# First attention of a decoder: compressed contexts as products of 64 rows into two banks, and the output added to the rows in every step

## The chip, the cores and the metric

The kernel runs on one core of a Trainium2 chip. The core has five engines that work side by side: PE multiplies matrices, DVE, ACT and POOL work on elements, SP starts transfers. PE writes to PSUM, a memory [...]; DVE and ACT read it from there. The metric is the device time of one execution in microseconds; lower is better. Matrices of f32 go through PE as two instructions for each product, each with a weight load (PEld) and a matmul (PE).

## The reference, cut to what matters

The program is a two-layer decoder in float32 on 16 blocks of 128 rows with 256 features. Only its first attention is touched. It has 16 heads of 128 features and two sources of values per head: a window of the rows around a query, and the entries, each a weighted mean of four neighbouring rows (32 entries per block), of which the best 8 are kept:

```python
entries = jnp.einsum('bcr,bcrh->bch', w_cmp, hidden_states.reshape(Bq, C, RATIO, HID))
cv = entries @ Wv + bv
...
ctx_sparse = jnp.einsum('bhsk,bhskd->bhsd', pw, v_g)
...
ctx_local = jnp.einsum('bhcqk,bhckd->bhcqd', pl, vw).reshape(Bq, NH, Sq, D)
merged = (ctx_sparse + ctx_local) * 0.5
out = merged.transpose(0, 2, 1, 3).reshape(Bq, Sq, NH * D) @ Wo + bo
```

The result is added to the input rows and normalized. The sum of both contexts and the product with Wo are what the change rearranges.

## The kernel before, in words

The first attention runs in 64 steps, one for each block b of 128 rows and each group hg of four heads, in the order b = 0, hg = 0 to 3, b = 1, and so on. A step's work is spread over four rounds of the loop at L486 and after, so that in one round PE works on four steps at once. PE's order is written out by hand (`manual_schedule` at L492 holds PE's instructions to the order of the program); the order on DVE, ACT and POOL is found by a planner that simulates costs.

In one round PE does, in this order:

1. `normed` with Wlk (L343, its product in `project`, L338): local keys of the new step, 512 columns;
2. `contexts` (L450) of the step that began three rounds ago;
3. `transposed` (L366): eight transposes of keys and queries of the step before, at L373;
4. `normed` with Wq (L338 again);
5. `output` (L461) of the step whose contexts were just made;
6. `scores` (L376), with a mask product at L380 and the scores at L384;
7. `weightsT` (L439): four transposes of the local weights (L442) and one of the compressed weights (L446), for the step that began two rounds ago;
8. `values` (L361): the product with Wlv;
9. now and then work on the entries (`entry_values` at L322 and others).

The compressed values of a block are kept in `cvz` (L271), a tile with four slots of 128 rows, one for each head. Slot h is zero but for rows 32h to 32h + 31, which hold the values of the 32 entries (written at L332). The compressed weights of four heads are transposed together: `pcT` (L445 to L448) has the 32 entries of head h in rows 32h to 32h + 31. A product of slot h with all 128 rows of pcT so picks the right head, because the other rows meet zeros.

`contexts` makes four accumulations of two products each into the tile `pm`, one PSUM bank with one buffer: for head h the local product (L454), then the compressed one (L455), both over all 128 rows. ACT then copies pm to `mT` in SBUF, times 0.5 (L457).

`output` multiplies mT by the group's rows of Wo (L465), four f32 products of 256 columns. They accumulate in the tile `po`, another bank, over all four groups of a block; only behind the last group DVE adds po to the block's rows `xs[b]` (L473). `output_bias` (L475), once in round 6, makes the part of the output that comes from the bias of the values, also in po's bank, and DVE and POOL add it to bo and all rows (L482, L484).

Of the kernel before, what the change touches and what calls it, by code (L numbers as in the profile page):

```python
# [18 lines left out]
F32 = mybir.dt.float32  # L19
# [3 lines left out]
AF = mybir.ActivationFunctionType  # L23
ALU = mybir.AluOpType
# [3 lines left out]
P = 128  # L28
HID = 256
# [19 lines left out]
def decoder(ctx: ExitStack, tc: tile.TileContext, w: dict, out: bass.AP):  # L49
    nc = tc.nc  # L50
# [12 lines left out]
    xs = [const.tile([P, HID], F32, name=f"x{t}") for t in range(NB)]  # L63
# [28 lines left out]
    def load_row(pool, ap, name, tag=None, bufs=None):  # L92

        n = ap.shape[0]
        kw = {} if tag is None else {"tag": tag, "bufs": bufs}
        t = pool.tile([P, n], F32, name=name, **kw)
        nc.gpsimd.dma_start(out=t, in_=ap.partition_broadcast(P))
        return t
# [73 lines left out]
    NH, D = 16, 128  # L172
    NC4 = P // 4
    NK = NC4 + P
    with ExitStack() as ph:
        pool = ph.enter_context(tc.tile_pool(name="l0a", bufs=1))
        wk = ph.enter_context(tc.tile_pool(name="l0a_k", bufs=2))
        ps = ph.enter_context(tc.tile_pool(name="l0a_ps", bufs=2, space=PSUM))
# [10 lines left out]
        wts, bias = {}, {}  # L189
# [16 lines left out]
        bo = load_row(pool, w["L0_attn_bo"], "bo0")  # L206
# [64 lines left out]
        cvz = [pool.tile([P, 4, D], F32, name=f"cvz{n}") for n in range(3)]  # L271
        for t in cvz:
            nc.gpsimd.memset(t, 0.0)

        def entry_logits(g):
            pl = ps.tile([P, NC4 * 4, 4], F32, tag="proj", name="pl")
            for k in range(2):
                nc.tensor.matmul(
                    pl.rearrange("p c r -> p (c r)"), lhsT=wcmp_b[:, k, :], rhs=xT[g][:, k, :], start=k == 0, stop=k == 1
                )  # L280
            lg = wk.tile([P, P, 4], F32, tag="big0", name="lg", bufs=1)
            nc.vector.tensor_scalar(lg, pl, bcmp, None, ALU.add)
            return lg
# [165 lines left out]

        def contexts(b, st):  # L450

            pm = ps.tile([P, 4, P], F32, tag="pm", name="pm", bufs=1)
            for h in range(4):
                nc.tensor.matmul(pm[:, h, :], lhsT=st["Wlv"][:, h, :], rhs=st["plT"][:, h, :], start=True, stop=False)  # L454
                nc.tensor.matmul(pm[:, h, :], lhsT=cvz[b % 3][:, h, :], rhs=st["pcT"], start=False, stop=True)  # L455
            st["mT"] = wk.tile([P, 4, P], F32, tag="mT", name="mT")
            nc.scalar.activation(st["mT"], pm, AF.Copy, scale=0.5)  # L457

        outs = {}

        def output(b, hg, st):  # L461
            if hg == 0:
                outs[b] = ps.tile([P, HID], F32, tag="po", name="po", bufs=1)
            for h in range(4):
                nc.tensor.matmul(  # L465
                    outs[b],
                    lhsT=st["mT"][:, h, :],
                    rhs=wts["Wo", hg][:, h, :],
                    start=hg == 0 and h == 0,
                    stop=hg == 3 and h == 3,  # L470
                )
            if hg == 3:
                nc.vector.tensor_tensor(xs[b], xs[b], outs.pop(b), ALU.add)  # L473

        def output_bias():  # L475

            pb = ps.tile([P, HID], F32, tag="po", name="pb", bufs=1)
            for h in range(NH):
                rep = wk.tile([P, P], F32, tag="blv_b", name="blv_b")
                nc.gpsimd.tensor_copy(rep, blv[:, h : h + 1].to_broadcast([P, P]))  # L480
                nc.tensor.matmul(pb, lhsT=rep, rhs=wts["Wo", h // 4][:, h % 4, :], start=h == 0, stop=h == NH - 1)
            nc.vector.scalar_tensor_tensor(bo, pb, 0.5, bo, ALU.mult, ALU.add)  # L482
            for t in range(NB):
                nc.gpsimd.tensor_tensor(xs[t], xs[t], bo, ALU.add)  # L484

# [5 lines left out]

        with tc.manual_schedule(engines={mybir.EngineType.PE}):  # L492
            lgs = {0: entry_logits(0)}
            entry_weights(lgs[0])
            for k in range(2):
                entry_sums(0, lgs[0], k)
            for n in range(len(steps) + 6):
# [5 lines left out]
                if fourth:  # L503
                    contexts(fourth[0], fourth[2])
# [12 lines left out]
                if fourth:  # L517
                    output(*fourth)
                if n == 6:
                    output_bias()  # L520
# [9 lines left out]
                g, r = (n + 10) // 16, (n + 10) % 16  # L530
                if 1 <= g < NG:
                    if r == 0:
                        lgs[g] = entry_logits(g)
                    elif r == 1:
                        entry_weights(lgs[g])
                    elif r in (2, 3):
                        entry_sums(g, lgs[g], r - 2)
                    elif r == 4:
                        cks[g] = entry_keys(g)
                    elif r == 6:  # L540
                        entry_keysT(g, cks.pop(g))
# [9 lines left out]
    with ExitStack() as ph:  # L551
# [174 lines left out]
        ps = ph.enter_context(tc.tile_pool(name="l0x_ps", bufs=1, space=PSUM))  # L726
# [225 lines left out]
        def put_out(gp, js, at):  # L952

            if 0 in js:
                pys[gp] = ps.tile([P, 2, HID], F32, tag="misc", name="py")
            output(gp, js, pys[gp])
            for u in range(2):
                if 4 * u + 3 in js:
                    later(at + 1, "DVE", add_output, 2 * gp + u, pys[gp][:, u])
            if 7 in js:  # L960
                later(at + 1, "POOL", norm_pair, gp)
# [82 lines left out]
        with tc.manual_schedule(engines=set(ordered)):  # L1044
            for n in range(len(steps) + 9):
# [11 lines left out]
                for part in range(2):  # L1057
# [8 lines left out]
                    gp, r = n // 16, n % 16  # L1066
                    if part == 1 and 0 < gp <= LAST and r >= 8:
                        ffn_half(gp - 1, r - 8, 1, at)
                    for hh in range(2):

                        q = n - 3 if (n - 3) % 2 == 1 else n - 4
# [260 lines left out]
    with ExitStack() as ph:  # L1332
        pool = ph.enter_context(tc.tile_pool(name="l1a", bufs=1))
        wk = ph.enter_context(tc.tile_pool(name="l1a_k", bufs=2))
        ps = ph.enter_context(tc.tile_pool(name="l1a_ps", bufs=1, space=PSUM))
# [37 lines left out]
        with tc.manual_schedule(engines={mybir.EngineType.PE}):  # L1373
# [4 lines left out]
            for n in range(len(steps) + 16):  # L1378
# [3 lines left out]
                if n in (5, 7):  # L1382
                    q = NB // 2 - 2 + n // 7
# [17 lines left out]
                t, r = n // 4, n % 4  # L1401
# [14 lines left out]
    with ExitStack() as ph:  # L1416
# [3 lines left out]
        ps = ph.enter_context(tc.tile_pool(name="l1x_ps", bufs=1, space=PSUM))  # L1420
# [47 lines left out]
        with tc.manual_schedule(engines={mybir.EngineType.PE}):  # L1468
# [8 lines left out]
            for n in range(len(steps) + 14):  # L1477
# [7 lines left out]
                t, r = n // 2, n % 2  # L1485
# [30 lines left out]
    with ExitStack() as ph:  # L1516
        wk = ph.enter_context(tc.tile_pool(name="l1f_k", bufs=2))
        ps = ph.enter_context(tc.tile_pool(name="l1f_ps", bufs=2, space=PSUM))

        def shares(g, i):  # L1520

            t = wk.tile([P, G], F32, tag="share", name="sh", bufs=6)
            at = 0
            while at < P:
                e = (i * P + at) // IE
                n = min(P - at, (e + 1) * IE - i * P - at)
                nc.sync.dma_start(out=t[at : at + n], in_=share[g][e, :].partition_broadcast(n))
                at += n
            return t

        def gated(g, rows, gate, up, sh=None):

            pgu = []
            for wt, tag in ((gate, "gate"), (up, "up")):
                pp = ps.tile([P, G], F32, tag=tag, name=tag)
                for k in range(2):
                    nc.tensor.matmul(pp[:rows], lhsT=wt[:, k, :], rhs=xT[g][:, k, :], start=k == 0, stop=k == 1)  # L1537
                pgu.append(pp)
            h = wk.tile([P, G], F32, tag="h", name="h", bufs=NI + 3 + 3)
            nc.scalar.activation(h[:rows], pgu[0][:rows], AF.Silu)  # L1540
            nc.vector.tensor_tensor(h[:rows], h[:rows], pgu[1][:rows], ALU.mult)  # L1541
            if sh is not None:
                nc.vector.tensor_tensor(h, h, sh, ALU.mult)
            return h

        for g in range(NG):
            parts = []
            for i in range(3):
                at, rows = i * P, min(P, IS - i * P)
                wsh = moe_w["sh"]  # L1550
                h = gated(g, rows, wsh[:, :, at : at + rows], wsh[:, :, IS + at : IS + at + rows])
                parts.append((h, moe_w["sd"][:rows, i, :], rows))
            for i in range(NI):
                at = slice(i * P, (i + 1) * P)
                h = gated(g, P, moe_w["g"][:, :, at], moe_w["u"][:, :, at], shares(g, i))
# [8 lines left out]
            for i4 in range(4):  # L1564
                t = 4 * g + i4
                py = ps.tile([P, HID], F32, tag="py", name="py")
                for n, (h, wt, rows) in enumerate(parts):
                    nc.tensor.matmul(  # L1568
                        py, lhsT=h[:rows, i4 * P : (i4 + 1) * P], rhs=wt, start=n == 0, stop=n == len(parts) - 1
# [59 lines left out]
```

## Time and profile before

| | |
|---|---|
| median of 3 runs | 2725.06 us (2724.89 to 2730.54) |
| profiled execution, its own time | 2732.66 us |
| its span, first to last instruction | 2730.9 us |
| mean granted TensorE clock | 0.974 |
| busy over the span: PE, PEld, DVE, ACT, POOL | 92%, 55%, 70%, 54%, 44% |
| contexts, L454 and L455: records of PE | 512 each, mean 277 ns |
| output, L465: records of PE | 512, mean 380 ns |
| addition of the output, L473 on DVE | 16, mean 414 ns |
| copy of the contexts, L457 on ACT | 64, mean 591 ns |

The profile names an instruction by engine and line; the operands are given by the program's names. A matmul's record lasts longer than the time for which it keeps the next one off, since matmuls are pipelined: the duration of one is told by its record, the room that it takes by the distance to the next start. In the rows, 128\*128 is the part of the array that a matmul uses (rows\*columns), behind it stand the elements of its output. PEclk, the granted clock, is a share of full speed.

### The profile page before, as it was taken

What the parts mean: (1) busy time and instruction counts of PE and PEld (TensorE: products, weight loads), DVE (VectorE), ACT (ScalarE), POOL (GpSimd) and SP (SyncE); (2) the same over time, 40 slices, a digit from 0 to 9 for tenths busy, and PEclk for the clock granted to TensorE, in tenths of its full rate; (3) what the DMA queues carried; (4) which work ended last, traced back from release to release, by engine and by line L of the source; (5) the groups of instructions that cost most, each with busy time, mean ns of one, the idle gap of its engine ahead of it and who ended that gap; (6) DMA issues with size and microseconds to landing.
All of it is one profiled execution on the core that took longest, in us unless ns stands there. A gap on an engine that the chain in (4) does not pass through costs nothing. (4 is left out here: it accounts for less than half of the span.)

```text
span 2730.9 us, 39531 instructions
## 1 busy us (share of the span) xinstructions
PE 2518.5 (92%) x13877; PEld 1493.5 (55%) x13908; DVE 1902.3 (70%) x4353; ACT 1473.7 (54%) x2778; POOL 1215.0 (44%) x1336
## 2 busy tenths in 40 slices
PE   6999999999986789988998888999988899999998
PEld 3677777777764133433433335666655546564746
DVE  5677777877757999999999963777777742324232
ACT  3455555555543888887887872555554531313120
POOL 5644544444436888888888873233132200000000
PEclk9999999999998899999999999999999999999999
DMA  7000000000011555655665562100100021111120
GB/s 226 1 1 1 1 1 1 1 1 1 1 50 29 106 116 111 128 122 107 119 125 110 113 136 97 55 2 2 42 16 11 2 63 47 54 39 60 34 67 10
DMA packets 360182, 150.82 MB, mean 55 GB/s; under 512 B 294576, under 2 KB 341136, under 8 KB 359472
## 3 DMA queue, kind: packets, MB, share of 16 engines
q1 hardware_dynamic: 358592, 144.49, 22.8%
q0 software_dynamic: 1392, 3.81, 0.6%
q8 instruction: 110, 1.80, 0.3%
q14 instruction: 88, 0.72, 0.1%
HBM read 74.71 MB, written 2.23 MB: 28 GB/s over the span
## 5 line engine op out<-in xcount | busy, mean ns | idle before, releaser
L786 POOL CAST aT<-at 128x2048 bf16<-128x2048 uint8 x256 | 480.9, 1894 | 91.5 <-DMA at<-a 88.6
L774 ACT ACTIVATE a<-e,snl 128x2048 uint8<-128x2048 f32 x256 | 510.7, 1996 | 3.5
L753 DVE TENSOR_SCALAR_CACHE_REDUCE e<-s,qs,smx 128x1024 f32<-128x1024 f32 x256 | 335.0, 1334 | 16.9 <-PE s L746 15.9
L753 DVE TENSOR_SCALAR_CACHE_REDUCE e<-s,qs 128x1024 f32<-128x1024 f32 x256 | 319.8, 1280 | 36.7 <-PE s L746 31.2
L796 PE MATMUL o<-aT,vq 128*32 128x512 bf16 x1024 | 262.8, 391 | 3.1 <-POOL aT L786 3.1
L746 PE MATMUL s<-kT,qT 64*128 64x512 bf16 x1024 | 191.0, 397 | 31.8 <-DVE e L753 28.7
L1541 DVE TENSOR_TENSOR h<-h,up 128x512 f32<-128x512 f32 (+1 forms) x100 | 68.7, 687 | 193.1 <-PE up L1537 189.4
L1540 ACT ACTIVATE h<-gate 128x512 f32<-128x512 f32 (+1 forms) x100 | 59.7, 597 | 220.1 <-PE gate L1537 219.9
L796 PEld LDWEIGHTS <-vq 128*32 128x32 bf16 x1024 | 85.5, 98 | 163.6 <-issue 89.4
L1537 PE MATMUL gate<-xT,w_L_ffn_w1g 128*128 128x512 f32 x352 | 167.7, 595 | 0.0
L1537 PE MATMUL up<-xT,w_L_ffn_w1u 128*128 128x512 f32 x352 | 165.4, 592 | 0.0
L1251 DVE TENSOR_REDUCE amx<-sc 128x8 f32<-128x1024 f32 x96 | 116.7, 1216 | 64.9 <-PE sc L1242 64.7
L1568 PE MATMUL py<-w_L_ffn_w2T,h 128*128 128x256 f32 x704 | 154.6, 379 | 0.0
L1254 ACT ACTIVATE pr<-pr 128x1024 f32<-128x1024 f32 x96 | 101.6, 1059 | 88.3 <-DVE pr L1253 88.3
L1263 ACT COPY prT<-tp 128x512 f32<-128x512 f32 x192 | 104.3, 584 | 76.7 <-PE tp L1262 76.3
L868 PE MATMUL gu<-xT,wgu 128*128 128x256 f32 x448 | 135.4, 427 | 9.2 <-ACT xT L160 4.3
L1568 PEld LDWEIGHTS py<-w_L_ffn_w2T,h 128*128 128x128 f32 x704 | 133.7, 190 | 18.3
L408 ACT ACTIVATE pls<-sc,lm,rms_rs 128x128 f32<-128x128 f32 x256 | 113.8, 454 | 21.6 <-DVE lm L404 21.6
L338 PE MATMUL proj<-Wlk,xT 128*128 128x512 f32 x256 | 121.1, 595 | 3.2 <-DVE ck L306 1.2
L338 PE MATMUL proj<-Wq,xT 128*128 128x512 f32 x256 | 122.0, 599 | 0.9 <-DVE raw_Wlk L347 0.9
L465 PE MATMUL po<-Wo,mT 128*128 128x256 f32 x512 | 121.2, 380 | 1.4 <-ACT mT L457 1.4
L1253 DVE TENSOR_TENSOR pr<-sc,amx 128x1024 f32<-128x1024 f32 x96 | 117.0, 1219 | 5.7
(313 smaller groups left out, 5378.9 us busy)
## 6 DMA issues: line engine op xcount, KB each, us to landing
wgu<-in_L_ffn_gu SPq DMA_DIRECT2D x112, 128.0 KB
sh<-share SPq DMA_DIRECT2D x32, 256.0 KB
at<-a SPq DMA_TRANSPOSE x256
sh<-share SPq DMA_DIRECT2D x16, 224.0 KB
sh<-share SPq DMA_DIRECT2D x16, 192.0 KB
w_L_ffn_w1g<-in_L_ffn_w1g SPq DMA_DIRECT2D x1, 2816.0 KB
w_L_ffn_w1u<-in_L_ffn_w1u SPq DMA_DIRECT2D x1, 2816.0 KB
w_L_ffn_w2T<-in_L_ffn_w2T SPq DMA_DIRECT2D x1, 2816.0 KB
```

What stands on the lines that cost most here:

```text
L338: nc.tensor.matmul(pp.rearrange("p h d -> p (h d)"), lhsT=xTt(b, k), rhs=wts[nm, hg][:, k, :], start=k == 0, stop=k == 1)
L465: nc.tensor.matmul(outs[b], lhsT=st["mT"][:, h, :], rhs=wts["Wo", hg][:, h, :], start=hg == 0 and h == 0, stop=hg == 3 and h == 3,)
L746: nc.tensor.matmul(s[hh][:, c, :], lhsT=qT[t % 4][r, i, :], rhs=kT[r, i, at : at + G], start=True, stop=True)
L753: nc.vector.tensor_scalar(st["e"][hh][:, half, :], s[hh].rearrange("p a b -> p (a b)"), qs[2 * gp + u][:, 2 * i + hh : 2 * i + hh + 1], No ...
L774: nc.scalar.activation(a.bitcast(U8), st["e"][hh].rearrange("p a b -> p (a b)"), AF.Exp, bias=st["nm"][:, hh : hh + 1], accum_out=groups[g ...
L786: nc.gpsimd.tensor_copy(aT[:, :, hh, u * P : (u + 1) * P].rearrange("p (b j) q -> p b j q", j=2), st["at"][hh].bitcast(U8).rearrange("p b ...
L796: nc.tensor.matmul(o[r : r + 32].rearrange("p a b -> p (a b)"), lhsT=vq[:, n, 32 * i : 32 * i + 32], rhs=aT[:, n].rearrange("p a b -> p (a ...
L868: nc.tensor.matmul(ffn_ps[q][:, n, :], lhsT=wt[:, k, :], rhs=xT[q // 2][:, k, at], start=k == 0, stop=k == 1)
L1251: nc.vector.tensor_reduce(mx, sc, AX.X, ALU.max)
L1253: nc.vector.tensor_tensor(pr, sc, bc(mx, 2, P), ALU.subtract)
L1537: nc.tensor.matmul(pp[:rows], lhsT=wt[:, k, :], rhs=xT[g][:, k, :], start=k == 0, stop=k == 1)
L1568: nc.tensor.matmul(py, lhsT=h[:rows, i4 * P : (i4 + 1) * P], rhs=wt, start=n == 0, stop=n == len(parts) - 1)
```

## The change

It has two parts that share one tile.

A tile `acc` of two banks takes the place of `pm` and `po`. In each bank the first half belongs to pm (two heads of 128 columns each), and the second half of bank 1 is po.

In `contexts` the heads come in two rounds, j = 0 with heads 0 and 2 and j = 1 with heads 1 and 3. A round makes the two local products (heads 0 and 2 go to different banks), then the two compressed ones. Of these each uses only the 64 rows in which its head's entries lie: rows 0 to 63 for heads 0 and 1, rows 64 to 127 for heads 2 and 3. The two products of a round so use different row halves of PE's array and different banks.

[...]`output` no longer accumulates over the four groups. It starts and ends its accumulation in every step, and DVE adds po to the rows in each of the 64 steps, not in 16.

```diff
+        acc = ps.tile([P, 2, 2, 2, P], F32, name="acc", bufs=1)
+        pm, po = acc[:, :, 0], acc[:, 1, 1].rearrange("p j q -> p (j q)")
...
-            pm = ps.tile([P, 4, P], F32, tag="pm", name="pm", bufs=1)
-            for h in range(4):
-                nc.tensor.matmul(pm[:, h, :], lhsT=st["Wlv"][:, h, :], rhs=st["plT"][:, h, :], start=True, stop=False)
-                nc.tensor.matmul(pm[:, h, :], lhsT=cvz[b % 3][:, h, :], rhs=st["pcT"], start=False, stop=True)
+            for j in range(2):
+                heads = (j, 2 + j)
+                for h in heads:
+                    nc.tensor.matmul(pm[:, h // 2, j], lhsT=st["Wlv"][:, h, :], rhs=st["plT"][:, h, :], start=True, stop=False)
+                for h in heads:
+                    r = slice(64 * (h // 2), 64 * (h // 2) + 64)
+                    nc.tensor.matmul(pm[:, h // 2, j], lhsT=cvz[b % 3][r, h, :], rhs=st["pcT"][r, :], start=False, stop=True)
             st["mT"] = wk.tile([P, 4, P], F32, tag="mT", name="mT")
-            nc.scalar.activation(st["mT"], pm, AF.Copy, scale=0.5)
-
-        outs = {}
+            nc.scalar.activation(st["mT"].rearrange("p (b j) q -> p b j q", b=2), pm, AF.Copy, scale=0.5)
 
         def output(b, hg, st):
-            if hg == 0:
-                outs[b] = ps.tile([P, HID], F32, tag="po", name="po", bufs=1)
             for h in range(4):
                 nc.tensor.matmul(
-                    outs[b],
+                    po,
                     lhsT=st["mT"][:, h, :],
                     rhs=wts["Wo", hg][:, h, :],
-                    start=hg == 0 and h == 0,
-                    stop=hg == 3 and h == 3,
+                    start=h == 0,
+                    stop=h == 3,
                 )
-            if hg == 3:
-                nc.vector.tensor_tensor(xs[b], xs[b], outs.pop(b), ALU.add)
+            nc.vector.tensor_tensor(xs[b], xs[b], po, ALU.add)
 
         def output_bias():
-            pb = ps.tile([P, HID], F32, tag="po", name="pb", bufs=1)
...
-                nc.tensor.matmul(pb, lhsT=rep, rhs=wts["Wo", h // 4][:, h % 4, :], start=h == 0, stop=h == NH - 1)
-            nc.vector.scalar_tensor_tensor(bo, pb, 0.5, bo, ALU.mult, ALU.add)
+                nc.tensor.matmul(po, lhsT=rep, rhs=wts["Wo", h // 4][:, h % 4, :], start=h == 0, stop=h == NH - 1)
+            nc.vector.scalar_tensor_tensor(bo, po, 0.5, bo, ALU.mult, ALU.add)
```

## The prediction

> **What bounds the kernel now.** I read the table of busy times by stage first, then PE's own waits, then PE's instructions in order of time. The change lies in the first attention only, which runs to about 808 us. Its steady part, from 120 to 790 us:
>
> ```profile
> 120.00:790.00 670.00, 665.84 (x3452) 480.69 (x3451) 520.20 (x1851) 371.84 (x1052) 316.20 (x435) 1.00 0.00 1
> ```
>
> The columns are length, then busy time and instructions of PE, PEld (weight loads), DVE, ACT and POOL, then granted clock and DMA. PE is busy 665.84 of 670 us, DVE 520.20 (78%), no DMA. A busy PE may still be a waiting PE, so the second view is all that PE's matmuls waited for in that stretch (us in total, times, longest):
>
> ```profile
> PE pm L455 <- DVE pcT L448: 1.6, 1, 1.6
> PE pm L454 <- ACT plT L444: 1.4, 1, 1.4
> PE proj L338 <- DVE ck L306: 1.2, 3, 0.4
> ```
>
> 4.2 us in 670: PE's list of instructions is the time. The third view is one step of that list (start, us, engine, line):
>
> ```profile
> 448.57 1.88 PE L338 MATMUL proj<-Wlk,xT 128*128 128x512 f32 x4
> 450.28 0.38 PE L454 MATMUL pm<-plT,raw_Wlv 128*128 128x128 f32 x2
> 450.50 0.39 PE L455 MATMUL pm<-pcT,cvz 128*128 128x128 f32 x2
> 450.73 0.39 PE L454 MATMUL pm<-plT,raw_Wlv 128*128 128x128 f32 x2
> ...
> 451.85 0.39 PE L455 MATMUL pm<-pcT,cvz 128*128 128x128 f32 x2
> 452.07 0.60 PE L373 MATMUL tp_qk<-ident,raw_Wlk 128*128 128x128 f32 x4
> 452.50 0.60 PE L373 MATMUL tp_qk<-ident,raw_Wq 128*128 128x128 f32 x4
> ```
>
> The time to the next start counts here, not the duration, since matmuls overlap. One f32 product is two records. A 512-column record holds PE for (450.28 - 448.57)/4 = 0.43 us, so 128 columns stream in 0.107 us. The contexts hold it for 452.07 - 450.28 = 1.79 us, 16 records at 0.112; half of that, 0.89 us, are the compressed ones of L455. Each record's weights are loaded under the record before, so loads cost nothing here. A step, from these contexts to the next (461.73), is 11.45 us, and 64 steps are some 730 us.
>
> **The change part by part.**
>
> *Compressed contexts as pairs of 64 rows.* Do two products in different row halves of the array run at once, and what does it cost to go there and back? The second attention, later in this kernel, does the same thing in f32 with 32-row operands into two banks:
>
> ```profile
> 1716.79 0.59 PE L1238 MATMUL sc<-causal,ident 128*128 128x512 bf16 x2
> 1717.31 1.13 PE L1242 MATMUL sc<-kz,qkT 32*128 32x512 f32 x4
> 1718.37 1.08 PE L1272 MATMUL o<-prT,vz 128*32 128x128 f32 x32
> ...
> 1722.14 1.13 PE L1242 MATMUL sc<-kz,qkT 32*128 32x512 f32 x4
> 1723.20 1.09 PE L1262 MATMUL tp<-ident,pr 128*128 128x128 f32 x8
> 1724.13 1.03 PE L1301 MATMUL py<-z_L_attn_WoT,oT 128*128 128x256 f32 x4
> ```
>
> Four 512-column records in a row would hold PE for 4 x 0.43 = 1.72 us; they hold it for 1.06. Two at a time is 0.86, so they do run in pairs, and 0.20 us is left. Its parts: the two bf16 records before stream for half of 0.43 each (in the first attention L380's 320 bf16 columns hold PE for 0.14 us, from 444.94 to 445.08), from 1716.79 to 1717.22, but L1242 starts at 1717.31, so PE stands still for 0.09 us when the shape of the array changes. The rest is a weight load that is no longer hidden:
>
> ```profile
> L1242 PE MATMUL sc<-kz,qkT x256: 587/640/692, 1695.5 to 1959.4; 32*128 32x512 f32 x128
> ```
>
> The longest (692 ns) are the first pair behind a change of shape, the shortest (587) the second pair, whose weights came in under the first: 0.105 us for a load in the open. Then 0.105 + 0.86 + 0.09 = 1.06. The way back is in the same rows: L1262's eight transposes hold PE for 1724.13 - 1723.20 = 0.93 us, against 8 x 0.109 = 0.87 in the first attention (two groups of four from 452.07 to 452.94), so their first load costs 0.06.
>
> Per step the new order is: two full products, a pair, two full products, a pair, then transposes. That is four changes of shape.
> - Removed: eight records of 0.112 = 0.89 us. Put in their place: two pairs, each two records deep, 4 x 0.107 to 0.112 = 0.43 to 0.45. Saved: 0.45 us.
> - Added: four stops of 0.095 (the 0.09 above with its rounding, which reaches 0.10) = 0.38 us; open loads of 0.105 before each pair and before the second full products, and of 0.06 before the transposes = 0.375 us. Together 0.755 us.
> - Net 0.755 - 0.45 = +0.30 us per step, and 64 steps give **+19.5 us**. All of it lies on the bound, as PE has no idle time in a step that could take it. The ends: 0.29 with pairs at 0.107, 0.35 with all four loads at 0.105: 19 to 22 us.
>
> Two rules of the Trainium skill are weighed here. "TensorE: Matmul & The Clock Gate", Part 3, puts a pack of tiles at one matmul's duration plus about 4 ns for each tile. By it alone the change saves 64 x 0.45 = 29 us; the trace bears out the concurrency but not the price. Against the change speaks "TensorEngine Tiling (Array Packing)", Key Properties: going to another tiling mode drains the engine. It gives no figure; the rows do, and four drains in a step cannot be left out. For the loads, the same TensorE page (Part 2, LDWEIGHTS) lets them be pulled ahead of matmuls in flight into a background buffer. If that held across a change of shape, only the drains were left, 4 x 0.095 - 0.45 = -0.07 us per step, -4.5 us in all. The 692 against 587 ns say that it doesn't, and I follow the row.
>
> *Output added in every step.* The matmuls of L465 stay the same 8 records, with other start and stop flags. DVE gets 48 more additions of L473:
>
> ```profile
> L473 DVE TENSOR_TENSOR x<-x,po x16: 412/414/420, 98.6 to 806.8; 128x256 f32<-128x256 f32 x16
>   PE po L465: 5.1, 1
> ```
>
> 48 x 0.414 = 19.9 us of DVE. The second line is how long DVE stood idle ahead of it: once, at the stage's end. In the other 15 places DVE was still busy when the product was done, so the addition waits for nobody. I cost it at nothing. The cover is DVE's own slack: 150 us idle in the 670, or 2.5 us of an 11.45 us step. Behind the addition in DVE's queue stand the scores' operations. Their first consumer on PE are the transposes of the weights one step later: in the step shown POOL ends the weights (L437) at 453.91 and PE transposes them at 457.75, 3.8 us of cover. The copy of pcT ends at 448.37 and the contexts read it from 450.50, 2.1 us. 0.41 us fits into each. If the cover were gone the price is 19.9 us.
>
> *One tile of two banks for pm and po.* The contexts of a step now also wait for the addition of the step before, as both lie in bank 1. On PE all that follows stands behind that wait. In the step shown an addition (L473, from 445.74) ends at 446.15; the next contexts begin at 450.28, 4.1 us of cover, hence nothing. The ACT copy to mT (L457, 0.60 us) reads as many elements from two banks; no row has a two-bank read of that form, so between -0.1 and +0.3 us, and I take nothing: it ends at 452.87, 1.8 us ahead of the output at 454.66. output_bias keeps its order, one wait each way as before. Other stages are not touched; that DVE, ACT and POOL are ordered by a planner can shift them by a few us either way.
>
> The sum: the profiled execution took 2732.66 us, 2730.9 of span and 1.8 around it. Its span becomes 2730.9 + 19.5 = 2750.4. It was 7.6 us above the median of the runs (2725.06), within 2.2 us of their highest. The difference is the same from the median: 2725.06 + 19.5 = **2744.6 us**.
>
> **The rivals.**
>
> *Pairs that do not pair.* If the two halves ran one after the other, 4 x 0.107 = 0.43 us per step come on top: +0.73 x 64 = 47 us, 2772. If only the second record of one head overlapped with the first of the other, half of that, 2758. Against it: the same f32 form in the second attention pairs both records. For it: those stream 512 columns, and here a load is as long as the stream.
>
> *DVE takes over.* If DVE's extra 19.9 us showed in full, 2764.5; with a third of it 2751. For it: 78% busy, and sums that feed POOL and then PE. Against: the 2 to 4 us of cover above, longer still if PE's steps grow.
>
> *The other side: loads hidden across the change of shape.* Place: the first load of each of the four sections. Price: with 0.11 us per change of shape the balance is even (0.45/4); the drain alone is 0.095. With all loads hidden the time is 2725.06 - 4.5 = 2720.6, with the drains gone too 2725.06 - 29 = 2696. Against it stand the first records of L1242, and a further place, where a 64-row group comes between f32 products:
>
> ```profile
> 1200.53 0.61 PE L746 MATMUL s<-kT,qT 64*128 64x512 bf16 x4
> 1201.07 1.13 PE L868 MATMUL gu<-xT,wgu 128*128 128x256 f32 x4
> ```
>
> Two pairs of 512 bf16 columns stream in 0.43 us and hold PE for 0.54: 0.11 is paid there again.
>
> **How the numbers follow.** A measurement here can tell about 0.2%, 5.5 us, from no change. My own case, switches at the trace's price and DVE hidden, gets 0.75 (2737 to 2755 by itself); pairs that fail 0.08, DVE or the shared bank in PE's way 0.09, hidden loads 0.08. The range of 2733 to 2763 leaves out the hidden loads and the wholly serial pairs, and takes in half-serial pairs and most of what DVE could cost. Hidden loads give faster 0.05 and same 0.03; the low end of my own case gives another 0.02 of same. So faster 0.05, same 0.05, slower 0.90.
>
> **What would show it.** In the changed profile, per step: contexts that hold PE for 1.79 + 0.25 to 0.3 us and the transposes after them 0.06 more; the records of the compressed products in two kinds, the first of each pair about 0.1 us longer; a step of 11.75 us instead of 11.45; PE's waits in the stage still a few us; 64 additions at L473 with next to no idle time ahead of them. The forecast is wrong if the compressed records start one after the other, if their first loads begin under the full products, or if PE waits for DVE's addition or for pcT in every step.

## The result, and the profile after

The changed kernel takes 2748.18 us (median of 4 runs, 2744.98 to 2754.29), the kernel before 2725.01; the ratio is 1.0076 with a 95% interval of 1.006 to 1.0093. Forecast were 2744.6 us, a ratio of 1.0072. Ratios and intervals, here and below, are those on record for the fast runs and not quotients of the medians (here 1.0085); the only slow run, 6333.97 us in the experiment with both pairs together, is left out of them. The profiled execution took 2747.84 us, with a span of 2746.1.

The same views as before, now of the changed kernel, whose lines have moved: L459 is the local product of the contexts, L462 the compressed one, L376 the transposes, L475 the addition of the output. The row of busy times for 120 to 790 us:

```profile
120.00:790.00 670.00, 665.99 (x3365) 458.33 (x3366) 521.71 (x1840) 368.81 (x1024) 311.05 (x429) 0.99 0.00 1
```

PE is as full as it was, and all that its matmuls waited for from 120 to 806 us is again a few us:

```profile
PE acc L462 <- DVE pcT L451: 1.6, 1, 1.6
PE acc L459 <- DVE x L475: 1.3, 1, 1.3
PE proj L341 <- DVE ck L309: 1.2, 3, 0.4
```

So the time is still the length of PE's list. One step of it (start, us, engine, line), with the rows at which the transposes and the step of the kernel before ended ahead of it:

```profile
452.94 1.88 PE L338 MATMUL proj<-Wq,xT 128*128 128x512 f32 x4
461.73 0.38 PE L454 MATMUL pm<-plT,raw_Wlv 128*128 128x128 f32 x2
```

```profile
450.09 0.61 PE L459 MATMUL acc<-plT,raw_Wlv 128*128 128x128 f32 x4
450.63 0.49 PE L462 MATMUL acc<-pcT,cvz 64*128 64x128 f32 x4
451.05 0.71 PE L459 MATMUL acc<-plT,raw_Wlv 128*128 128x128 f32 x4
451.69 0.49 PE L462 MATMUL acc<-pcT,cvz 64*128 64x128 f32 x4
452.11 0.66 PE L376 MATMUL tp_qk<-ident,raw_Wlk 128*128 128x128 f32 x4
...
453.04 1.88 PE L341 MATMUL proj<-Wq,xT 128*128 128x512 f32 x4
...
461.83 0.61 PE L459 MATMUL acc<-plT,raw_Wlv 128*128 128x128 f32 x4
```

The contexts hold PE from 450.09 to 452.11, 2.02 us against 1.79, the transposes from 452.11 to 453.04, 0.93 against 0.87, and a step is 461.83 - 450.09 = 11.74 us against 11.45. Four compressed records now fit into 0.42 us (450.63 to 451.05), of which about 0.2 is their own streaming. What the rest is can be read in part from the durations (ns, shortest/median/longest) of the compressed products; below them stands the addition on DVE, with DVE's idle time ahead of it:

```profile
L462 PE MATMUL acc<-pcT,cvz x512: 272/373/579, 58.8 to 824.0; 64*128 64x128 f32 x171
```

```profile
L475 DVE TENSOR_TENSOR x<-x,acc x64: 406/414/422, 65.8 to 827.1; 128x256 f32<-128x256 f32 x64
...
  PE acc L468: 9.8, 3
```

Nearly all records are of one of two kinds, half of them 272 and half 373 ns. A product is two records, and those of a pair run side by side: the first record of each head, behind the change of shape, is 0.101 us longer than the second, by the weight load in the open. The few longer ones (up to 579 ns) lie in stretches of low clock (last section). DVE stood idle ahead of the addition only three times in 64.

How much of it the stage accounts for is seen where the next stage's first product starts. Before:

```profile
813.74 2.07 PE L618 MATMUL pv<-ctxT,w_L_xattn_Wkv 128*128 128x512 f32 x2 [0.67 <-ACT xT L127]
```

and after:

```profile
833.92 2.07 PE L619 MATMUL pv<-ctxT,w_L_xattn_Wkv 128*128 128x512 f32 x2 [0.68 <-ACT xT L127]
```

That is 20.2 us in the first attention. Of these 1.3 us lie ahead of the first contexts, which start at 58.24 us instead of 56.90; they are not explained. The other 18.8 are the 64 steps at 0.29 to 0.30 us. The two spans differ by 15.2 us, so later stages, which the change doesn't touch, were 5 us quicker in this execution; in a second profiled execution of the changed kernel (below) they were 2 us slower than before. In the nine profiled executions of this document they took from 1907 to 1919 us.

### The profile page after: what moved, and what is told of

It reads as the page before. It is cut to its first block, busy times and chain, and to the rows that moved or that the text cites. A ratio compares the mean times of both kernels' runs of the same rounds, so it can differ in the third digit from the quotient of the medians.

```text
span 2746.1 us, 39618 instructions
## 1 busy us (share of the span) xinstructions
PE 2533.5 (92%) x13877; PEld 1481.0 (54%) x13908; DVE 1917.3 (70%) x4401; ACT 1479.4 (54%) x2778; POOL 1215.5 (44%) x1336
## 5 line engine op out<-in xcount | busy, mean ns | idle before, releaser
L468 PE MATMUL acc<-Wo,mT 128*128 128x256 f32 x512 | 121.2, 379 | 1.4 <-ACT mT L464 1.4
```

## The experiments

The theory is that of the prediction. The rivals are that DVE's additions or the shared tile make the loss, or that the pairs save nothing. The time of each run stands beside that of the kernel before, measured anew together with it. Edits are against the changed kernel unless another is named.

### Full rows again

```diff
-                    r = slice(64 * (h // 2), 64 * (h // 2) + 64)
-                    nc.tensor.matmul(pm[:, h // 2, j], lhsT=cvz[b % 3][r, h, :], rhs=st["pcT"][r, :], start=False, stop=True)
+                    nc.tensor.matmul(pm[:, h // 2, j], lhsT=cvz[b % 3][:, h, :], rhs=st["pcT"], start=False, stop=True)
```

> The changed kernel with its compressed products over all 128 rows again, as before; the order of the heads, the shared tile and the addition in every step stay. Theory (the loss is four changes of the array's shape per step, less what the pairs save; additions and the shared tile cost nothing): the time of the kernel before, 2725 us, within 3 us, and a step of 11.45 us. Rival (DVE's 48 additions or the wait in the shared bank make the loss): 2740 to 2748 us, as the changed kernel.

Measured: 2726.46 us against 2730.39, a ratio of 0.9989 (0.998 to 0.9998). A step in its list of PE:

```profile
450.01 0.61 PE L459 MATMUL acc<-plT,raw_Wlv 128*128 128x128 f32 x4
450.46 0.61 PE L461 MATMUL acc<-pcT,cvz 128*128 128x128 f32 x4
...
451.80 0.60 PE L376 MATMUL tp_qk<-ident,raw_Wlk 128*128 128x128 f32 x4
```

The contexts are back at 1.79 us, though the other order of heads, the shared tile and all 64 additions are still there. The whole loss comes with the products of 64 rows; the first rival falls. The 0.1% that it is quicker than the kernel before is not explained: the next stage starts 0.6 us earlier (813.18), and the rest lies in later stages.

### Eight changes, no pairs

```diff
-            for j in range(2):
-                heads = (j, 2 + j)
-                for h in heads: ...local...
-                for h in heads: ...compressed, 64 rows...
+            for h in range(4):
+                r = slice(64 * (h // 2), 64 * (h // 2) + 64)
+                nc.tensor.matmul(pm[:, h // 2, h % 2], lhsT=st["Wlv"][:, h, :], rhs=st["plT"][:, h, :], start=True, stop=False)
+                nc.tensor.matmul(pm[:, h // 2, h % 2], lhsT=cvz[b % 3][r, h, :], rhs=st["pcT"][r, :], start=False, stop=True)
```

> The changed kernel with each head by itself: local product, then its 64-row product, eight changes of shape per step and no pairs. Theory: eight stops of 0.095 = 0.76, open loads of 4 x 0.105 + 3 x 0.105 + 0.06 = 0.80, nothing saved: +1.55 us per step, +99 us, 2824 us (2815 to 2830). Rival (pairs save nothing and a change of shape costs 0.08 us): +0.64 per step, 2766 us.

Measured: 2827.38 us, a ratio of 1.0357 (1.0337 to 1.0377), which is 97 us of 2730.

```profile
447.99 0.38 PE L458 MATMUL acc<-plT,raw_Wlv 128*128 128x128 f32 x2
448.30 0.48 PE L459 MATMUL acc<-pcT,cvz 64*128 64x128 f32 x2
448.71 0.49 PE L458 MATMUL acc<-plT,raw_Wlv 128*128 128x128 f32 x2
449.13 0.49 PE L459 MATMUL acc<-pcT,cvz 64*128 64x128 f32 x2
...
451.21 0.66 PE L376 MATMUL tp_qk<-ident,raw_Wlk 128*128 128x128 f32 x4
```

One product of two records holds PE for 0.42 us when it stands between two changes (448.71 to 449.13), 0.2 of which is its own work. One 64-row head takes 0.41 us here (448.30 to 448.71), and in the changed kernel a pair of two heads takes the same 0.42: the second head of a pair is free. Both terms of the sum, the price of a change and the gain of a pair, are thus seen apart, and the rival with worthless pairs and cheap changes (2766 us) falls.

### Two changes, pairs of 64 rows

To put all four compressed products behind one another, each head got a bank of its own (in these tiles 512 columns of f32), in one tile of four banks that also holds the scores (`sc`) and the output.

```diff
-        acc = ps.tile([P, 2, 2, 2, P], F32, name="acc", bufs=1)
-        pm, po = acc[:, :, 0], acc[:, 1, 1].rearrange("p j q -> p (j q)")
+        acc = ps.tile([P, 4, G], F32, name="acc", bufs=1)
+        pm, po = acc[:, :, 3 * P : 4 * P], acc[:, 3, 0:HID]
...
-            sc = ps.tile([P, 2, G], F32, tag="sc", name="sc", bufs=1)
+            sc = acc[:, 0:2]
...
+            for h in range(4): ...local product into pm[:, h]...
+            for h in (0, 2, 1, 3):
+                r = slice(64 * (h // 2), 64 * (h // 2) + 64)
+                nc.tensor.matmul(pm[:, h], lhsT=cvz[b % 3][r, h, :], rhs=st["pcT"][r, :], start=False, stop=True)
...
```

> All four local products first, each head in a bank of its own (two of them in the unused columns of the scores' banks), then both pairs of 64 rows: two changes of shape per step, not four. Theory: two stops of 0.095, open loads of 0.105 and 0.06, less 0.45 us for the pairs: -0.095 us per step, 64 steps -6 us, 2719 us. Rival (pairs save nothing, a change of shape costs 0.08 us): 2725 + 64 x 0.16 = 2735 us. If the scores' banks are read too late for the contexts, PE's waits show it, at L459 or its like.

Measured: 2808.96 us, a ratio of 1.0299 (1.0279 to 1.0319), 82 us slower where 6 us of gain were expected. The profile says why. PE's list around the contexts, and DVE's addition of the same step:

```profile
443.66 1.05 PE L457 MATMUL acc<-plT,raw_Wlv 128*128 128x128 f32 x8
444.65 0.72 PE L460 MATMUL acc<-pcT,cvz 64*128 64x128 f32 x8
445.29 0.66 PE L376 MATMUL tp_qk<-ident,raw_Wlk 128*128 128x128 f32 x4
...
447.94 1.89 PE L466 MATMUL acc<-Wo,mT 128*128 128x256 f32 x8
450.93 0.30 PE L383 MATMUL acc<-mask,ident 128*128 128x320 bf16 x1 [1.10 <-DVE x L473]
```

```profile
450.13 0.42 DVE L258 TENSOR_TENSOR raw_Wq<-rope_a,rope_b 128x256 f32<-128x256 f32 x1
450.46 0.41 DVE L473 TENSOR_TENSOR x<-x,acc 128x256 f32<-128x256 f32 x1
```

The contexts did what the theory says: 445.29 - 443.66 = 1.63 us against 1.79, and with 0.06 more for the transposes a gain of 0.10 per step. But PE now stands before the scores (L383) until DVE has added the output (L473), since both lie in one tile and their order is kept. Eight records of the output hold PE for 1.72 us, to 449.66, and the scores start at 450.93: 1.27 us per step, 64 steps 81 us. Less the gain that is 75 of the 82 us; some waits are longer (up to 6.9 us), and what else makes up the rest is not shown. The addition takes 0.41 us; the rest is DVE's own queue, in which a sum of squares (L353, from 449.53) and the rope of the queries (L258) stand first. That the tile makes PE wait is the reading of this profile; the run with two tiles below tests it.

### Four products of 32 rows

```diff
-            for h in (0, 2, 1, 3):
-                r = slice(64 * (h // 2), 64 * (h // 2) + 64)
+            for h in range(4):
+                r = slice(NC4 * h, NC4 * h + NC4)
```

(against the kernel of the last run)

> As the run with two changes of shape, but each compressed product uses only the 32 rows of its own head, so that four products in four quarters of the array and four banks can run at once. Theory: the eight records of 0.112 become two of 0.107, 0.68 us saved, for two stops of 0.095 and open loads of 0.105 and 0.06: -0.33 us per step, -21 us, 2704 us. Rival (no more than two run at once): 2719 us, as with two pairs; (none at once): 2725 + 64 x 0.32 = 2745 us.

Measured: 2800.01 us, a ratio of 1.0256 (1.0238 to 1.0275). It has the same wait at the scores. Its contexts:

```profile
449.21 1.05 PE L457 MATMUL acc<-plT,raw_Wlv 128*128 128x128 f32 x8
450.19 0.50 PE L460 MATMUL acc<-pcT,cvz 32*128 32x128 f32 x8
450.63 0.44 PE L376 MATMUL tp_qk<-ident,raw_Wlk 128*128 128x128 f32 x2
```

1.42 us against 1.79, less 0.06 for the transposes: 0.31 us per step gained in the contexts, where 0.33 were expected. The eight records hold PE for 0.44 us, no longer than the four of a pair (0.42): four products do run at once. Whether the time follows when the wait is gone was the next question.

### Four products of 32 rows, two tiles

The edit is against the kernel of the last run. The scores (`sc`) become `scp`, and the products of heads 0 and 1 go there too.

```diff
-        acc = ps.tile([P, 4, G], F32, name="acc", bufs=1)
-        pm, po = acc[:, :, 3 * P : 4 * P], acc[:, 3, 0:HID]
+        acc = ps.tile([P, 2, G], F32, name="acc", bufs=1)
+        scp = ps.tile([P, 2, G], F32, name="scp", bufs=1)
+        pms, po = [x[:, :, 3 * P : 4 * P] for x in (scp, acc)], acc[:, 1, 0:HID]
...
-            nc.scalar.activation(st["mT"], pm, AF.Copy, scale=0.5)
+            for i in range(2):
+                nc.scalar.activation(st["mT"][:, 2 * i : 2 * i + 2, :], pms[i], AF.Copy, scale=0.5)
```

> Four products of 32 rows at once again, but the scores' two banks and the two banks with the output are separate tiles (the contexts are copied in two ACT instructions of 256 columns). Theory (the +70 us of the run with one tile of four banks are PE's wait at the scores for DVE's addition, which lies in the same tile; the contexts themselves gain 0.31 us per step): that wait is gone, a step is 11.45 - 0.31 = 11.14 us, and the time is 20 us below the kernel before of the same call, a ratio of 0.9927. Rival (the wait belongs to the banks or to a late DVE, not to the tile): PE still waits about 1.1 us at the scores, and the ratio stays near 1.025.

Measured: 2729.4 us against 2729.16, a ratio of 0.9994 (0.9984 to 1.0004). The wait at the scores is gone, so it belonged to the tile, and a step is 459.76 - 448.62 = 11.14 us, as expected:

```profile
448.62 0.61 PE L458 MATMUL scp<-plT,raw_Wlv 128*128 128x128 f32 x4
449.07 0.61 PE L458 MATMUL acc<-plT,raw_Wlv 128*128 128x128 f32 x4
449.61 0.38 PE L461 MATMUL scp<-pcT,cvz 32*128 32x128 f32 x2
449.62 0.38 PE L461 MATMUL acc<-pcT,cvz 32*128 32x128 f32 x2
...
450.04 0.66 PE L377 MATMUL tp_qk<-ident,raw_Wlk 128*128 128x128 f32 x4
...
459.76 0.61 PE L458 MATMUL scp<-plT,raw_Wlv 128*128 128x128 f32 x4
```

Yet the 20 us are not there. PE's waits, from 120 to 830 us:

```profile
PE scp L458 <- ACT pls L412: 12.2, 5, 5.2
```

Two heads' contexts lie in the scores' banks and must wait until ACT has read the scores of the step before. In most steps it has; in five, where DVE has work on the entries or the stage runs out, it has not. The next stage's first product starts at 810.92 us, 2.8 us earlier than before, so some 17 us are missing. Over the whole stage the contexts wait for 13.6 us, against 4.6 in the kernel before: 9 us. Most of the rest is the clock: the granted clock is about one half in four stretches, each behind such a wait, in which the kernel before has 0.84 or 1.00 (last section). From these clocks (7 us at 0.56, twice 4 us at 0.57 and 7 us at 0.51, against 7 us at 0.84) some 9 us are lost, an estimate.

### Both pairs together, in two banks

The changed kernel ends a head's accumulation before the other head of its bank starts one. With this kept, the order can still have both pairs side by side, if the second pair opens its accumulations and the local products close them:

```diff
...
+            for f, heads, start in (
+                (local, (0, 2), True), (compressed, (0, 2), False), (compressed, (1, 3), True), (local, (1, 3), False)
+            ):
+                for h in heads:
+                    f(h, start)
```

> The changed kernel, two banks and pairs of 64 rows, with the second pair moved next to the first: local products of heads 0 and 2, both pairs (the second opens its accumulation), local products of heads 1 and 3. Two changes of shape per step instead of four. Theory: two stops of 0.095, two open loads of 0.105, less 0.45 us: -0.05 us per step, a step of 11.40 us, 3 us below the kernel before of the same call (ratio 0.997 to 1.001), and 23 us below the changed kernel. Rival (the loss does not come from the number of changes): as the changed kernel, ratio 1.0076.

Measured: 2723.53 us against 2729.16, a ratio of 0.9977 (0.9968 to 0.9986): 0.2% faster than the kernel before, as expected, and faster than the changed one. A step of its list, and the durations of the compressed products:

```profile
459.81 0.61 PE L457 MATMUL acc<-plT,raw_Wlv 128*128 128x128 f32 x4
460.35 0.71 PE L463 MATMUL acc<-pcT,cvz 64*128 64x128 f32 x8
460.99 0.71 PE L457 MATMUL acc<-plT,raw_Wlv 128*128 128x128 f32 x4
461.54 0.60 PE L376 MATMUL tp_qk<-ident,raw_Wlk 128*128 128x128 f32 x4
```

```profile
L463 PE MATMUL acc<-pcT,cvz x512: 272/272/579, 57.4 to 799.2; 64*128 64x128 f32 x171
```

Contexts of 1.73 us, 0.06 less than before, with transposes that find their weights loaded: 64 x 0.06 = 4 us, and the next stage's first product starts at 809.70, 4.0 us earlier. The same eight compressed records as in the changed kernel, with two changes of shape fewer, turn a loss of 20 us in the stage into a gain of 4. Two pairs hold PE for 0.64 us (460.35 to 460.99), one pair 0.42: the second pair costs no more than its two records' streaming, and the median record is now the short one. So the price is that of the change of shape, and not of products of 64 rows as such.

### The changed kernel once more

> The changed kernel itself, timed in as many rounds as the experiments, so that its loss can be set beside theirs. Theory (0.30 us per step, 64 steps, nothing else): 19.5 us above the kernel before of the same call, a ratio of 1.006 to 1.008; and beside the run with full rows, which has all of the change but the pairs, 1.007. Rival (the additions of the output take part in the loss): nearer to 1.010.

Measured: 2751.69 us against 2728.31, a ratio of 1.0079 (1.0059 to 1.0099). In this execution the next stage's first product starts at 833.43, 19.7 us later than before. The run with full rows lies 0.0090 below in ratio, some 25 us. That is above the 0.007 expected and nearer to the rival's 0.010; the two intervals together leave room for the 19.5 of the sum. It doesn't speak for the additions, since both runs have them. In the profiles the next stage starts 20.25 us later here than with full rows (833.43 and 813.18); the rest lies in later stages.

## Why the prediction was right, point by point

- *PE's list is the time, and nothing hides an addition to it.* Right: busy 665.99 of 670 us after, waits of 4.1 us.
- *The price per step.* 0.30 us were summed up, 0.29 measured (11.74 against 11.45 us), of which 0.23 in the contexts, just under the 0.25 to 0.3 that were to show it, and 0.06 in the transposes. The stop was put at 0.095 us: the first four local records hold PE for 0.54 us (450.09 to 450.63), with full rows behind them for 0.45 (450.01 to 450.46). The open load was put at 0.105 and is 0.101 in the records of L462. 64 x 0.29 = 18.6 us; the stage lost 20.2 and 19.7 us in two executions, about 1 us of it ahead of the first contexts. The terms fit one by one, so the sum is not right by luck.
- *The pairs.* Two heads take the 0.42 us that one takes by itself. The doubt that a load as long as the stream could spoil it was empty.
- *Loads hidden across the change of shape*, the rival on the other side: every run with a change of shape has the longer first records (272 against 373 ns in the changed kernel).
- *The additions and the shared tile at nothing.* Right for this change, as the run with full rows shows. The price that the prediction put on lost cover would have been too low, had it been lost at the scores. It counted 0.41 us per step, 19.9 us in all; in the run with two changes, where PE did come to wait for the addition, each step lost 1.27 us, since the addition stands behind DVE's other work.
- *The whole time.* 19.5 us were forecast; the medians differ by 23.2 and the spans by 15.2 and 21.6. The stage agrees to within 1 us. The rest lies outside it, where the profiled executions differ among themselves by up to 12 us; that the medians' difference is 3.7 us above the forecast is put down to this scatter and not shown.

## What to carry to other kernels

Packing small products side by side in PE's array was paid for here by the number of times that the array changes its shape, not by the number of products: 0.095 us of standstill and up to 0.1 us of open weight load each time, together about as much as two f32 records of 128 columns. What PE does in the standstill, no profile here shows. So gather all packed products of a step behind one change, and count the changes before counting what the packing saves. When tiles are merged to make room, look at which instructions come to wait for each other through the tile alone, and price such a wait with all that stands in the other engine's queue.

## What the runs showed of the hardware

About some waits of PE the granted clock is low for a few us. In the run with four products in two tiles PE stands for 5.2 us, to 133.10, and for 1.7 us, to 321.82. Its rows behind these waits, and the first of the same stretches in the changed kernel:

```profile
133.00:140.00 7.00, 6.90 (x28) 5.11 (x29) 3.38 (x8) 3.18 (x8) 3.19 (x4) 0.56 0.01 2
323.00:327.00 4.00, 4.00 (x19) 2.85 (x20) 2.42 (x6) 2.35 (x5) 3.19 (x4) 0.57 0.00 0
```

```profile
133.00:140.00 7.00, 5.63 (x22) 4.37 (x23) 5.38 (x25) 4.80 (x14) 2.91 (x4) 0.53 0.01 2
```

The four local records at 133.10 hold PE for 1.02 us, where the same four take 0.45 at 448.62. If the low clock comes of the wait, which no run here tests apart, a wait costs more than its own length. The length alone doesn't tell how much: the changed kernel has 0.53 with waits of only 1.3 and 1.6 us at that place, the kernel before 0.84 in the same 7 us with 1.4 and 1.6. And the run with two changes, in which PE waits for 1.10 us in every step, keeps a clock of 1.00 from 400 to 540 us. What decides it stays open.
